# Layer 0's denominators and normed tokens turned in 32x32 squares, and its projection put off by one block

## The chip, the cores and the metric

The kernel runs on one core of one Trainium2 chip. Its engines are PE (TensorE: matmuls and the transposes that go through PSUM), DVE (VectorE), ACT (ScalarE), POOL (GpSimd) and SP, which here only issues DMAs. The metric is the device time of one execution in microseconds (us).

## The reference, cut to what matters

The input is x of 4 images, 128 channels, 64 x 64 pixels: 4 x 128 x 4096 in float32. Layer 0 is an attention over pixels with 64 inner channels, layer 1 a causal attention over the same 4096 tokens with 128 channels, and then a recurrence over the tokens.

```python
# layer 0, per image, xf = x.reshape(128, 4096)
q, k, v = wq @ xf, wk @ xf, wv @ xf                  # 64 x 4096 each
att = softmax(k.T @ q, axis=-1)                      # 4096 x 4096
x = x + wo @ (att @ v.T).T
# layer 1, tokens t = x.T (4096 x 128)
n = layernorm(t)
t = t + softmax(causal((n Wq) (n Wk).T / sqrt(128))) (n Wv)
w = batchnorm(layernorm(t) W)                        # statistics over all images and tokens
y[0] = 0;  y[i] = sigmoid(w[i] + y[i-1] V.T);  t = t + y
```

## The kernel before, in words

Batch by batch (b, the image), layer 0 and then layer 1 go over 8 blocks g of 512 rows of the attention (tokens). For each block the keys are walked in items, two 128-key tiles at a time: 16 items for each block of layer 0, 2 to 16 for a block of layer 1. The main loop (L822) has one slot s per item. In a slot stand, in this order of the program text: `scores` of item s (PE into the PSUM tile s_ps, two buffers; ACT then writes the exponentials p, four buffers), `values` of item s-2 (PE adds p times v, or times the normed tokens, into acc, one buffer), some work at a block's end, `sums` of item s (DVE adds p into dsum, the running denominators), and one piece of work that is due. The scores and values of layer 0 are matmuls on quarters of the array (64 x 64), those of layer 1 use the whole of it (128 x 128).

At a block's last `values` ACT copies acc out (half), DVE adds its parts up to agg (128 x 512, the unnormalized result) and folds dsum into den (128 x 512, keys in partitions, still to be summed over the partitions). Then the loop calls `rows` (L812: takes the query rows for the block after the next: L533 on PE and L535 on DVE for layer 1, a token load on SP for layer 0), pops one entry of the list `fill` (L836), and pushes the block's finishing chain, `finish0` or `finish1`, onto `waiting`. A chain is a generator: each of its steps yields after how many slots it is due, and one due step is taken in a slot (L841), the longest due first. Where none is due, a step of `side` (keys and values of the next batch) is taken. The order on each engine is then fixed when the program is built; the planner that does it may move an instruction past others that don't depend on it, so the order of the trace isn't always that of the text.

Finishing a block of layer 0 takes: `project` (L538), which turns den into one reciprocal per token (rec), multiplies agg by wo on PE (o_ps, L562) and adds it, times rec, to the tokens in xs (four instructions on DVE, L567); `normed` (L571), the layernorm of four token tiles on DVE with a power on POOL (L450), into xh; and `transposed` (L587), which turns xh into xhT, channels in partitions, by four PE transposes (L591) and an ACT copy (L592). In `project` layer 0 turns den with four PE transposes (L557) and reduces them from PSUM (L558). Layer 1 does the same by 32x32 squares: one DVE transpose of all squares (L546), a reduce within the squares (L548, part), a matmul with the 0/1 matrix fold that adds the four partition groups (L549), and on DVE a product with the mask quarter and a reduce (L551, L554). PSUM tiles of `project`, `rows`, the keys and `transposed` share one tag, misc, with two buffers.

Layer 1 finishes in three steps, `first` (project, store of the tokens into x2, norm), `second` (the normed tokens turned on DVE in squares, L640, stored into DRAM as by_c by four DMAs, L645, and loaded as xhT by one, L649) and `third` (the matmul with wf, L653). Tiles agg and den live in the pool `work` (two buffers each).

Layer 0's tokens xhT and xh are what layer 1's `scores` and `values` multiply with: block g's are first read by `rows` and `scores` of layer 1's block g.

Of the kernel before, what the change touches and what calls it, by code (L numbers as in the profile page):

```python
# [9 lines left out]
F32 = mybir.dt.float32  # L10
AF = mybir.ActivationFunctionType
ALU = mybir.AluOpType
AX = mybir.AxisListType
PSUM = bass.MemoryType.PSUM

P = 128
BLK = 512
# [332 lines left out]
def fast_path(  # L350
# [21 lines left out]
    nc = tc.nc  # L372
# [5 lines left out]
    TPB = BLK // P  # L378
# [5 lines left out]
    S = nc.vector.STREAM_SQUARE_SIZE  # L384
    Q = P // S
# [4 lines left out]
    dram2 = ctx.enter_context(tc.tile_pool(name="dram2", bufs=2, space=bass.MemoryType.DRAM))  # L390
# [31 lines left out]
    ident = const.tile([P, P], F32, name="ident")  # L422
# [10 lines left out]
    fold = const.tile([P, P], F32, name="fold")  # L433
# [6 lines left out]
    quarter = const.tile([P, TPB, Q], F32, name="quarter")  # L440
# [15 lines left out]
    with tc.tile_pool(name="batch", bufs=1) as batch, tc.tile_pool(name="rows", bufs=2) as rowp, tc.tile_pool(  # L456
        name="prob", bufs=4
    ) as prob, tc.tile_pool(name="work", bufs=2) as wk, tc.tile_pool(name="stat", bufs=4) as stat, tc.tile_pool(
        name="ps_s", bufs=2, space=PSUM
    ) as ps_s, tc.tile_pool(name="ps_a", bufs=1, space=PSUM) as ps_a, tc.tile_pool(  # L460
        name="ps_m", bufs=2, space=PSUM
# [12 lines left out]
        bs = [Batch() for _ in range(B)]  # L474
# [60 lines left out]
            nc.vector.tensor_copy(r, ps)  # L535
            bs[b].next.append(r)

        def project(layer, b, g, agg, den):  # L538

            dp = misc("den_ps")  # L540
            rec = recs[:, layer, b, ts(g, TPB)]
            if layer:


                sq = wk.tile([P, TPB * Q, S], F32, tag="sq", name="sq")
                nc.vector.transpose(out=sq.rearrange("p a b -> p (a b)"), in_=den)  # L546
                part = stat.tile([P, TPB * Q], F32, tag="part", name="part")
                nc.vector.tensor_reduce(part, sq, AX.X, ALU.add)  # L548
                nc.tensor.matmul(dp[:, : TPB * Q], lhsT=fold, rhs=part, start=True, stop=True)  # L549
                own = stat.tile([P, TPB, Q], F32, tag="own", name="own")  # L550
                nc.vector.tensor_tensor(  # L551
                    own, dp[:, : TPB * Q].rearrange("p (j q) -> p j q", q=Q), quarter, ALU.mult
                )
                nc.vector.tensor_reduce(rec, own, AX.X, ALU.add)  # L554
            else:
                for j in range(TPB):
                    nc.tensor.transpose(dp[:, ts(j, P)], den[:, ts(j, P)], ident)  # L557
                nc.vector.tensor_reduce(rec, dp.rearrange("p (j k) -> p j k", k=P), AX.X, ALU.add)  # L558
            nc.vector.reciprocal(rec, rec)
            op = misc("o_ps")  # L560
            for j in range(TPB):
                nc.tensor.matmul(  # L562
                    op[:, ts(j, P)], lhsT=agg[:, ts(j, P)], rhs=wv1 if layer else wo2, start=True, stop=True
                )
            for j in range(TPB):
                t = xs[:, b, ds(g * BLK + j * P, P)]
                nc.vector.scalar_tensor_tensor(  # L567
                    t, in0=op[:, ts(j, P)], scalar=rec[:, j : j + 1], in1=t, op0=ALU.mult, op1=ALU.add
                )
# [17 lines left out]
        def transposed(src, dst, name, engine):  # L587

            ps = misc(name)
            for j in range(TPB):  # L590
                nc.tensor.transpose(ps[:, ts(j, P)], src[:, j], ident)  # L591
            engine(dst, ps)  # L592

        def in_range():

            r = recs.rearrange("p l b t -> p (l b t)")
            r2 = wk.tile([P, BLK], F32, tag="den", name="r2")[:, : 2 * B * NT]
            nc.vector.tensor_scalar(r2, r, LOW, None, ALU.is_ge)
            nc.vector.tensor_scalar(r, r, HIGH, None, ALU.is_le)
            nc.vector.tensor_tensor(r, r, r2, ALU.mult)  # L600
            nc.vector.tensor_reduce(good, r, AX.X, ALU.add)

        def finish0(b, g):

            agg, den = bs[b].agg, bs[b].den

            def norm():
                if g == 0:
                    bs[b].xh = batch.tile([P, NT, P], F32, tag="xh", name="xh")
                    bs[b].xhT = batch.tile([P, N], F32, tag="xhT", name="xhT")  # L610
                normed(b, g, bs[b].xh[:, ts(g, TPB)])

            yield 2, lambda: (project(0, b, g, agg, den), norm())
            fill.append(
                lambda: transposed(bs[b].xh[:, ts(g, TPB)], bs[b].xhT[:, ts(g, BLK)], "xhT_ps", nc.scalar.copy)
            )

        def finish1(b, g):
            agg, den = bs[b].agg, bs[b].den
            mem = {}  # L620
            final = b == B - 1 and g == NB - 1

            def first():
                project(1, b, g, agg, den)
                nc.sync.dma_start(
                    out=x2[b, ts(g, BLK)].rearrange("(j p) c -> p j c", p=P),
                    in_=xs[:, b, ts(g, BLK)].rearrange("p (j c) -> p j c", c=P),
                )
                mem["xh"] = wk.tile([P, TPB, P], F32, tag="xh2", name="xh2")
                normed(b, g, mem["xh"])  # L630

            def second():
                mem["xhT"] = wk.tile([P, BLK], F32, tag="xhT2", name="xhT2")
                if final:
                    transposed(mem["xh"], mem["xhT"], "xh2T_ps", nc.vector.tensor_copy)
                    return


                sq = wk.tile([P, Q, TPB, S], F32, tag="sqT", name="sqT")
                nc.vector.transpose(  # L640
                    out=sq.rearrange("p c j t -> p j c t"), in_=mem["xh"].rearrange("p j (c r) -> p j c r", r=S)
                )
                by_c = dram2.tile([Q, S, Q, P], F32, tag="by_c", name="by_c")
                for q in range(Q):
                    nc.sync.dma_start(  # L645
                        out=by_c[:, :, q].rearrange("c r k -> r c k"),
                        in_=sq[ts(q, S)].rearrange("r c j t -> r c (j t)"),
                    )
                nc.sync.dma_start(out=mem["xhT"], in_=by_c.rearrange("c r q k -> (c r) (q k)"))  # L649

            def third():
                wp = misc("wx_ps")
                nc.tensor.matmul(wp, lhsT=wf, rhs=mem["xhT"], start=True, stop=True)  # L653
                if b == B - 1 and g == NB - 1:
                    in_range()
                nc.vector.bn_stats(stats[:, b * NB + g], wp)  # L656

                to = xs[:, b, ts(g, BLK)]
                if final:
                    nc.scalar.copy(to.rearrange("p (s c) -> p s c", c=CPB), wp.rearrange("p (c s) -> p s c", s=STEPS))  # L660
                else:
                    nc.scalar.copy(  # L662
                        to.rearrange("p (s j q u) -> p s j q u", q=Q, j=TPB, s=STEPS),
                        wp.rearrange("p (q j u s) -> p s j q u", q=Q, j=TPB, s=STEPS),
                    )

            yield 1, first
            yield 3, second
            yield 1 if final else 4, third
# [121 lines left out]
        fill = []  # L791

        def push(slot, chain):
            step = next(chain, None)
            if step:
                waiting.append((slot + step[0], step[1], chain))
# [25 lines left out]
        for s in range(len(items) + SKEW + 16):  # L822
            if s < len(items):
                it = items[s]
                if it.first:
                    bs[it.b].rows = bs[it.b].next.pop(0)
                    if it.layer and it.g == 1 and it.b + 1 < B:
                        for m in range(NB // 2):
                            side += keys(it.b + 1, m)
                scores(it)  # L830
            if 0 <= s - SKEW < len(items):
                it = items[s - SKEW]
                values(it)
                if it.last:
                    rows()
                    if fill:  # L836
                        fill.pop(0)()
                    push(s, (finish1 if it.layer else finish0)(it.b, it.g))
            if s < len(items):
                sums(items[s])  # L840
            due = [w for w in waiting if w[0] <= s]  # L841
            if due:
                w = min(due, key=lambda w: w[0])
                waiting.remove(w)
                w[1]()
                push(s, w[2])
            elif side:
                side.pop(0)()
# [7 lines left out]
    with tc.tile_pool(name="xr", bufs=1) as xrp, tc.tile_pool(name="y", bufs=2) as yp, tc.tile_pool(  # L856
        name="ps_y", bufs=1, space=PSUM
# [21 lines left out]
        start = xrp.tile([P, B, NCH + 1], F32, name="start")  # L879
# [55 lines left out]
        for b in range(B):  # L935
# [3 lines left out]
            sq = yp.tile([P, NCH], F32, tag=f"y{b}", name="sq")  # L939
# [70 lines left out]
```

## Time and profile before

| | |
|---|---|
| median of 8 runs | 2144.36 us (2142.72 to 2146.3) |
| the profiled execution | 2142.87 us, span 2141.1 us, granted clock 0.994 |
| PE busy | 2093.4 us (98%) |
| DVE busy | 1467.0 us (69%) |
| ACT busy | 1008.4 us (47%) |
| four den transposes on PE, L557 | 128, 20.8 us busy |
| four token transposes on PE, L591 | 128, 20.4 us busy |
| reduce of the denominators from PSUM, L558 | 32, 21.9 us busy |
| copy of the tokens out of PSUM, L592 | 32, 19.0 us busy (ACT) |

The profile is that of one execution. Busy time is the time in which an engine has at least one instruction running; matmuls overlap, so the sum of their lengths is more than PE's busy time. A line of the timeline has the start in us, the length in us, the engine, the line of the kernel, the operation, the tiles written and read, the number of like instructions merged, and in brackets the time that the engine stood idle before it and which instruction ended that.

### The profile page before, as it was taken

What the parts mean: (1) busy time and instruction counts of PE and PEld (TensorE: products, weight loads), DVE (VectorE), ACT (ScalarE), POOL (GpSimd) and SP (SyncE); (2) the same over time, 40 slices, a digit from 0 to 9 for tenths busy, and PEclk for the clock granted to TensorE, in tenths of its full rate; (3) what the DMA queues carried; (4) which work ended last, traced back from release to release, by engine and by line L of the source; (5) the groups of instructions that cost most, each with busy time, mean ns of one, the idle gap of its engine ahead of it and who ended that gap; (6) DMA issues with size and microseconds to landing.
All of it is one profiled execution on the core that took longest, in us unless ns stands there. A gap on an engine that the chain in (4) does not pass through costs nothing. (4 is left out here: it accounts for less than half of the span.)

```text
span 2141.1 us, 30417 instructions
## 1 busy us (share of the span) xinstructions
PE 2093.4 (98%) x12016; PEld 925.6 (43%) x12016; DVE 1467.0 (69%) x2807; ACT 1008.4 (47%) x1098; POOL 104.2 (5%) x207
## 2 busy tenths in 40 slices
PE   6999999999999999999999999999999999999978
PEld 2333344444333344444333334444433334544446
DVE  3888875554788876554588887555488887654478
ACT  4666633333566643333466663333356664323255
POOL 0000010000000000000000001000000001000000
PEclk9999999999999999999999999999999999999989
DMA  7000022000000002100000002200000000110033
GB/s 227 2 1 2 1 60 57 18 15 15 16 1 1 2 18 71 35 25 15 16 1 2 1 1 59 59 15 15 15 16 1 1 2 6 40 30 15 15 162 159
DMA packets 65319, 64.99 MB, mean 30 GB/s; under 512 B 5648, under 2 KB 55056, under 8 KB 63120
## 3 DMA queue, kind: packets, MB, share of 16 engines
q1 hardware_dynamic: 63280, 62.41, 9.8%
q8 instruction: 96, 1.57, 0.3%
q10 hardware_dynamic: 1888, 0.56, 0.1%
q14 instruction: 55, 0.45, 0.1%
HBM read 33.85 MB, written 24.90 MB: 27 GB/s over the span
## 5 line engine op out<-in xcount | busy, mean ns | idle before, releaser
L744 DVE TENSOR_TENSOR dsum<-dsum,p 128x1024 f32<-128x1024 f32 x676 | 827.1, 1224 | 446.3 <-ACT p L720 320.4
L718 ACT ACTIVATE p<-s_ps,nshift 128x1024 f32<-128x1024 f32 x512 | 571.2, 1116 | 348.7 <-PE s_ps L704 328.8
L720 ACT ACTIVATE p<-s_ps 128x1024 f32<-128x1024 f32 (+2 forms) x288 | 274.2, 952 | 564.2 <-PE s_ps L713 542.5
L764 PE MATMUL acc<-p,v 64*64 64x512 f32 x4096 | 533.6, 591 | 1.7 <-ACT half L783 1.7
L704 PE MATMUL s_ps<-swap,kr 64*64 64x512 f32 x2048 | 529.2, 594 | 0.4 <-ACT p L718 0.4
L704 PE MATMUL s_ps<-kr 64*64 64x512 f32 x2048 | 529.2, 594 | 0.0
L713 PE MATMUL s_ps<-rows,xhT 128*128 128x512 f32 (+3 forms) x1152 | 503.3, 559 | 1.4 <-DVE rows L535 1.4
L772 PE MATMUL acc<-p,xh 128*128 128x512 f32 (+3 forms) x1152 | 501.7, 558 | 0.0
L772 PEld LDWEIGHTS acc<-p,xh 128*128 128x128 f32 x1152 | 216.2, 191 | 240.8 <-issue 231.4
L713 PEld LDWEIGHTS s_ps<-rows,xhT 128*128 128x128 f32 x1152 | 213.4, 190 | 241.9 <-issue 196.1
L764 PEld LDWEIGHTS acc<-p,v 64*64 64x64 f32 x4096 | 155.5, 133 | 285.1 <-issue 266.1
L704 PEld LDWEIGHTS s_ps<-swap,kr 64*64 64x64 f32 x2048 | 137.5, 133 | 132.8 <-issue 125.1
L704 PEld LDWEIGHTS s_ps<-kr 64*64 64x64 f32 x2048 | 137.6, 133 | 128.3 <-issue 123.7
L450 POOL TENSOR_TENSOR ln_rstd<-ln_var,mhalf 128x4 f32<-128x4 f32 x64 | 65.7, 1027 | 1205.0 <-DVE ln_var L579 1194.1
L752 DVE TENSOR_TENSOR dsum<-dsum,p 128x256 f32<-128x256 f32 (+1 forms) x120 | 55.8, 499 | 74.2 <-POOL p L724 74.2
L567 DVE SCALAR_TENSOR_TENSOR xs<-o_ps,recs,xs 128x128 f32<-128x128 f32 x256 | 72.4, 344 | 8.8 <-PE o_ps L562 3.1
L583 DVE TENSOR_SCALAR xh<-xs,ln_mv,ln_rstd 128x128 f32<-128x128 f32 x256 | 71.3, 342 | 2.2
L724 POOL TENSOR_SCALAR_AFFINE_SELECT p<-p 128x128 f32<-128x128 f32 x128 | 34.4, 292 | 665.6 <-ACT p L720 650.8
L576 DVE BATCH_NORM_STATS2 ln_st<-xs 128x6 f32<-128x128 f32 x256 | 63.5, 270 | 0.0
L742 DVE COPY dsum<-p 128x1024 f32<-128x1024 f32 x60 | 41.4, 690 | 31.8 <-ACT p L720 26.6
L662 ACT COPY xs<-wx_ps 128x512 f32<-128x512 f32 x31 | 18.1, 585 | 83.7 <-DVE stats L656 79.1
L909 DVE SCALAR_TENSOR_TENSOR z<-xs,scale,y_ps 128x256 f32<-128x256 f32 x108 | 48.6, 480 | 6.7 <-PE y_ps L907 5.5
(115 smaller groups left out, 1047.1 us busy)
## 6 DMA issues: line engine op xcount, KB each, us to landing
xs<-in_x SPq DMA_DIRECT2D x16, 512.0 KB, 7.3
xs<-in_xT SPq DMA_DIRECT2D x32, 256.0 KB, 3.2
x<-xs SPq DMA_DIRECT2D x32, 256.0 KB, 2.3
xr<-x SPq DMA_DIRECT2D x8, 1024.0 KB, 11.9
out_x<-xr SPq DMA_DIRECT2D x8, 1024.0 KB, 6.0
by_c<-sqT SPq DMA_DIRECT2D x124, 64.0 KB, 1.8
xhT<-by_c SPq DMA_DIRECT2D x31, 256.0 KB, 2.6
swap<-kr SPq DMA_DIRECT2D x32, 128.0 KB, 2.2
```

Of the source, the lines that this page charges most:

```text
L450: nc.gpsimd.tensor_tensor(y, var, mhalf[:, : y.shape[-1]], ALU.pow)
L567: nc.vector.scalar_tensor_tensor(t, in0=op[:, ts(j, P)], scalar=rec[:, j : j + 1], in1=t, op0=ALU.mult, op1=ALU.add)
L576: nc.vector.bn_stats(st[:, j], xs[:, b, ds(g * BLK + j * P, P)])
L583: nc.vector.tensor_scalar(dst[:, j], xs[:, b, ds(g * BLK + j * P, P)], mv[:, j, 0:1], y[:, j : j + 1], ALU.subtract, ALU.mult)
L704: nc.tensor.matmul(ps[c * M : c * M + M, off : off + n], lhsT=bs[it.b].kr[part, h, ds(t % (NT // 2) * P + c * M, M)], rhs=rows[h], start=True,
L713: nc.tensor.matmul(ps[:, off : off + n], lhsT=lhsT, rhs=rhs, start=True, stop=True)
L718: nc.scalar.activation(it.p[:, :off], ps[:, :off], AF.Exp, bias=nshift)
L720: nc.scalar.activation(it.p[:, :off], ps[:, :off], AF.Exp, scale=float(P) ** -0.5)
L744: nc.vector.tensor_tensor(flat, flat, it.p, ALU.add)
L752: nc.vector.tensor_tensor(den[:, h, q0:], den[:, h, q0:], it.p[:, o : o + n], ALU.add)
L764: nc.tensor.matmul(bt.acc[h * M : h * M + M, r], lhsT=bt.v[part, t], rhs=it.p[part, o : o + n], start=it.first, stop=it.last,)
L772: nc.tensor.matmul(bt.acc[:, 0, q0:], lhsT=bt.xh[:, t], rhs=it.p[:, o : o + n], start=it.first and h == 0, stop=it.last and h == 1,)
```

## The change

Layer 0 takes over layer 1's way of turning. `project` has one form for both layers, and its first half, the DVE transpose of den in squares and the reduce to part, becomes a function of its own, `folded`. The normed tokens of a layer-0 block are no more transposed by PE: DVE turns their 32x32 squares (`squares`, the code that layer 1 had in its `second`), four DMAs on SP's queue put these into a DRAM tile by_r (pieces of 32 tokens, 128 bytes), and four more load the rows of xhT from it.

The steps of `finish0` stand elsewhere. Before: project and norm together, due two slots behind the block's end, and the transposes at the next block's end (the entry in `fill`). After: `folded` due one slot behind the block's end; project at the next block's end (the entry in `fill`), and from there a new chain: norm due one slot later, `by_channels` (squares and the eight DMAs) two after that. At a block's end the chain of the block before is pushed ahead of the block's own. `finish1` calls the same functions with the same work as before.

```diff
+        def folded(den):
+            sq = wk.tile([P, TPB * Q, S], F32, tag="sq", name="sq")
+            nc.vector.transpose(out=sq.rearrange("p a b -> p (a b)"), in_=den)
+            part = stat.tile([P, TPB * Q], F32, tag="part", name="part")
+            nc.vector.tensor_reduce(part, sq, AX.X, ALU.add)
+            return part
+
-        def project(layer, b, g, agg, den):
+        def project(layer, b, g, agg, part):
             dp = misc("den_ps")
             rec = recs[:, layer, b, ts(g, TPB)]
-            if layer:
...
-            else:
-                for j in range(TPB):
-                    nc.tensor.transpose(dp[:, ts(j, P)], den[:, ts(j, P)], ident)
-                nc.vector.tensor_reduce(rec, dp.rearrange("p (j k) -> p j k", k=P), AX.X, ALU.add)
+            nc.tensor.matmul(dp[:, : TPB * Q], lhsT=fold, rhs=part, start=True, stop=True)
+            own = stat.tile([P, TPB, Q], F32, tag="own", name="own")
+            nc.vector.tensor_tensor(own, dp[:, : TPB * Q].rearrange("p (j q) -> p j q", q=Q), quarter, ALU.mult)
+            nc.vector.tensor_reduce(rec, own, AX.X, ALU.add)
             nc.vector.reciprocal(rec, rec)
...
+        def squares(src):
+            sq = wk.tile([P, Q, TPB, S], F32, tag="sqT", name="sqT")
+            nc.vector.transpose(out=sq.rearrange("p c j t -> p j c t"), in_=src.rearrange("p j (c r) -> p j c r", r=S))
+            return sq
...
-            yield 2, lambda: (project(0, b, g, agg, den), norm())
-            fill.append(
-                lambda: transposed(bs[b].xh[:, ts(g, TPB)], bs[b].xhT[:, ts(g, BLK)], "xhT_ps", nc.scalar.copy)
-            )
+            def by_channels():
+                sq = squares(bs[b].xh[:, ts(g, TPB)])
+                by_r = dram2.tile([S, Q, TPB, Q, S], F32, tag="by_r", name="by_r")
+                for q in range(Q):
+                    nc.sync.dma_start(
+                        out=by_r[:, :, :, q].rearrange("r c j t -> r (c j) t"),
+                        in_=sq[ts(q, S)].rearrange("r c j t -> r (c j) t"),
+                    )
+                for c in range(Q):
+                    nc.sync.dma_start(
+                        out=bs[b].xhT[ts(c, S), ts(g, BLK)], in_=by_r[:, c].rearrange("r j q t -> r (j q t)")
+                    )
+
+            def rest():
+                yield 1, norm
+                yield 2, by_channels
+
+            def first():
+                part = folded(den)
+
+                def second(s):
+                    project(0, b, g, agg, part)
+                    push(s, rest())
+
+                fill.append(second)
+
+            yield 1, first
...
-                project(1, b, g, agg, den)
+                project(1, b, g, agg, folded(den))
...
-                        fill.pop(0)()
+                        fill.pop(0)(s)
```

More of the change, by code (lines that the diff above doesn't have):

```diff
@@ L536, in rows1 @@
             bs[b].next.append(r)
-        def project(layer, b, g, agg, den):
+        def folded(den):
[5 more added lines that the diff above has]
+        def project(layer, b, g, agg, part):
             dp = misc("den_ps")
             rec = recs[:, layer, b, ts(g, TPB)]
-            if layer:
[L545 to L552, printed above, removed]
-                )
-                nc.vector.tensor_reduce(rec, own, AX.X, ALU.add)
-            else:
-                for j in range(TPB):
-                    nc.tensor.transpose(dp[:, ts(j, P)], den[:, ts(j, P)], ident)
-                nc.vector.tensor_reduce(rec, dp.rearrange("p (j k) -> p j k", k=P), AX.X, ALU.add)
+            nc.tensor.matmul(dp[:, : TPB * Q], lhsT=fold, rhs=part, start=True, stop=True)
+            own = stat.tile([P, TPB, Q], F32, tag="own", name="own")
+            nc.vector.tensor_tensor(own, dp[:, : TPB * Q].rearrange("p (j q) -> p j q", q=Q), quarter, ALU.mult)
+            nc.vector.tensor_reduce(rec, own, AX.X, ALU.add)
             nc.vector.reciprocal(rec, rec)
@@ L611, in norm @@
                 normed(b, g, bs[b].xh[:, ts(g, TPB)])
-            yield 2, lambda: (project(0, b, g, agg, den), norm())
-            fill.append(
-                lambda: transposed(bs[b].xh[:, ts(g, TPB)], bs[b].xhT[:, ts(g, BLK)], "xhT_ps", nc.scalar.copy)
-            )
+            def by_channels():
[20 more added lines that the diff above has]
+            yield 1, first
         def finish1(b, g):
@@ L636, in second @@
                     return
[L639 to L642, printed above, removed]
+                sq = squares(mem["xh"])
                 by_c = dram2.tile([Q, S, Q, P], F32, tag="by_c", name="by_c")
```

## The prediction

> **What bounds the kernel now.** I read the page's engine totals first, then the busy time per stretch, then PE, DVE and ACT in order of time through one layer-0 block end, then the same for layer 1, where the new form of the denominators already runs.
>
> The engine totals, and one layer-0 block of 16 items in the view of stretches (span, then PE, PEld, DVE, ACT, POOL busy, clock, DMA share, GB/s):
>
> ```profile
> PE 2093.4 (98%) x12016; PEld 925.6 (43%) x12016; DVE 1467.0 (69%) x2807; ACT 1008.4 (47%) x1098; POOL 104.2 (5%) x207
> 182.20:212.04 29.84, 29.84 (x274) 11.36 (x273) 24.98 (x41) 19.19 (x19) 1.01 (x1) 1.00 0.01 1
> ```
>
> PE never stops in the block, at full granted clock; DVE, 69% of the whole, is 84% busy here. So the two have to be set against each other per block, and not over the span.
>
> PE in order of time around a block end (start us, length, engine, line):
>
> ```profile
> 89.67 1.04 PE L764 MATMUL acc<-p,v 64*64 64x512 f32 x8
> ...
> 91.38 1.04 PE L764 MATMUL acc<-p,v 64*64 64x512 f32 x8
> 92.35 0.66 PE L591 MATMUL xhT_ps<-ident,xh 128*128 128x128 f32 x4
> ...
> 93.85 1.04 PE L764 MATMUL acc<-p,v 64*64 64x512 f32 x8
> ...
> 95.56 1.04 PE L764 MATMUL acc<-p,v 64*64 64x512 f32 x8
> 96.53 0.66 PE L557 MATMUL den_ps<-ident,den 128*128 128x128 f32 x4
> 97.03 1.06 PE L562 MATMUL o_ps<-wo,agg 128*128 128x128 f32 x8
> ...
> 98.92 1.04 PE L764 MATMUL acc<-p,v 64*64 64x512 f32 x8
> ```
>
> A plain slot takes 1.716 us (ACT's starts, 220.31 to 239.19, are eleven slots). The slot with the token transposes takes 2.47, so these cost PE 0.75. The slot with denominators and projection takes 3.36, so these cost 1.64, of which 0.98 is the projection (97.03 to 98.01, where the scores go on). Sixteen slots of 1.716 (27.46) and 2.39 make 29.85: nothing else is in the period, and PE sets it.
>
> DVE in the same kind of block (in brackets the idle time before, and its releaser):
>
> ```profile
> 210.03 0.69 DVE L788 TENSOR_TENSOR den<-dsum 128x512 f32<-128x512 f32 x1
> ...
> 212.20 1.23 DVE L744 TENSOR_TENSOR dsum<-dsum,p 128x1024 f32<-128x1024 f32 x1 [0.87 <-ACT p L718]
> ...
> 214.67 1.23 DVE L744 TENSOR_TENSOR dsum<-dsum,p 128x1024 f32<-128x1024 f32 x1 [0.64 <-ACT p L718]
> 216.38 1.23 DVE L744 TENSOR_TENSOR dsum<-dsum,p 128x1024 f32<-128x1024 f32 x1 [0.49 <-ACT p L718]
> ...
> 222.09 0.16 DVE L451 TENSOR_TENSOR ln_z<-ln_rstd 128x4 f32<-128x4 f32 x1 [1.12 <-POOL ln_rstd L450]
> ...
> 224.93 13.21 DVE L744 TENSOR_TENSOR dsum<-dsum,p 128x1024 f32<-128x1024 f32 x10
> 238.63 1.23 DVE L744 TENSOR_TENSOR dsum<-dsum,p 128x1024 f32<-128x1024 f32 x1 [0.49 <-ACT p L718]
> ```
>
> The idle times add to 3.61, so DVE needs 26.25 of 29.86. The ten sums back to back show it 3.5 us behind ACT (the sum at 224.93 takes a p that ACT ended at 221.42), catching up 0.4 us a slot (1.716 less 1.32).
>
> **What is removed and added, on PE.** In layer 1 the fold and the projection look so, with the transpose of the normed tokens on DVE:
>
> ```profile
> 397.93 0.29 PE L549 MATMUL den_ps<-part,fold 128*128 128x16 f32 x2
> 398.07 1.14 PE L562 MATMUL o_ps<-wv,agg 128*128 128x128 f32 x8
> ...
> 405.18 0.71 DVE L640 STREAM_TRANSPOSE sqT<-xh 128x512 f32<-128x512 f32 x1
> 405.81 1.18 DVE L744 TENSOR_TENSOR dsum<-dsum,p 128x1024 f32<-128x1024 f32 x1
> ```
>
> The fold takes 0.14 of PE there, with its weight loads hidden. Behind 64x64 work both loads (0.19 each) may show: 0.38 at most. I take 0.20, nearer the measured one. The moved projection stays 0.98. Going into 128x128 work shows 0.11 (96.42, the end of the eight L764 at 95.56 plus 0.86, to 96.53), and the first scores after it take 0.05 more; two such visits a block become one. New: 0.11 + 0.20 + 0.98 + 0.05 = 1.34 against 2.39: 1.05 us saved a block, period 28.80. Seven of a batch's eight blocks pay in layer 0: 28 x 1.05 = 29.4. The eighth is dealt with among layer-1 work, where four transposes cost 0.44 (299.86 to 300.30; 283.72 to 284.16): 0.44 + 0.44 - 0.14 = 0.74, times 4 = 3.0. Together 32.4 us.
>
> The token transposes also covered PE's wait for the copy of acc at a block end (0.42 idle at 63.94, the first block, where there are none). The projection, 1.34 long, now stands there, so that stays covered.
>
> **PSUM buffers of the misc tag (two).** At a batch's last two layer-0 ends the rows of layer 1 (L533) take one, den_ps the other, and o_ps must wait until DVE has copied the rows: in the trace the rows matmul is over at 242.59, the copy at 243.88. With o_ps straight behind, PE waits 1.1 (243.9 less 242.8). Where this happens today, the order steps around it: at 283.72 den_ps, then scores at 284.16, then o_ps at 285.67; here that costs one more visit, 0.16. Between 0.16 and 1.1, nearest the stepping around: 0.3, eight times, 2.4 us.
>
> **What is added on DVE.** Squares and reduce of den, 0.74 + 0.69 (430.45 to 431.19, and the reduce); own and its reduce 0.41 (398.69 to 399.10); squares of the tokens 0.63 (above); less the reduce from PSUM, 0.72 (98.10 to 98.82). Plus 1.75: 28.00 a block, inside PE's 28.80, if it waits for nothing. But DVE waits for POOL's power in every norm. Near the end of layer 0, where DVE is behind:
>
> ```profile
> 1827.45 1.22 DVE L744 TENSOR_TENSOR dsum<-dsum,p 128x1024 f32<-128x1024 f32 x1
> 1829.57 0.16 DVE L451 TENSOR_TENSOR ln_z<-ln_rstd 128x4 f32<-128x4 f32 x1 [0.90 <-POOL ln_rstd L450]
> 1827.62 1.91 POOL L450 TENSOR_TENSOR ln_rstd<-ln_var,mhalf 128x4 f32<-128x4 f32 x1 [9.56 <-DVE ln_var L579]
> ```
>
> A sum put into that wait began 0.17 before the power, which took 1.91 instead of 1.01, and DVE stood 0.90 all the same. Where the power began first (401.92, sum at 402.10) it took 1.01 and no wait was left. With DVE behind, the next p is always ready, so the sum will begin first: I charge 0.90 a block, 1.12 if nothing is put in. DVE: 28.90 to 29.12, above PE by 0.10 to 0.32.
>
> [...]
>
> Does that excess reach PE? There are four p buffers: ACT writes item k+4 once DVE has summed item k, 6.86 us after item k's start; less ACT's 1.12 and the sum's 1.29, DVE may be 4.45 late before ACT waits, and ACT has 1.4 to spare before PE does: 5.85. The new lag, from the end of the last p of a block (0): last sum 1.26, den 0.61, copy 0.69, squares and reduce 1.43, sum 1.14, agg 0.69, own to the four updates 1.72, sum 1.22, statistics 1.41, sum 1.22, 0.90, chain and xh 1.70, sum 1.30, squares 0.63 = 15.9; the p then due ended at 11.6 (6 x 1.716 + 1.34). Lag 4.3 to 4.5, under 5.85; the spare 1.4 takes up most of seven drifts of 0.10 to 0.32. What is left is 0 to 1.2 a batch: 0 to 5 us, I take 2.
>
> **Queues and the delay.** ACT loses 32 copies of 0.59: off the path. SP gets eight DMAs a block: four stores at 0.44 (1.76 for the like four), four loads at 0.34, 3.1 of 28.8. Behind them on SP stand the token loads two blocks ahead, the x2 stores and by_c; the loads wait there for the stores to land. The nearest store (64 KB in 512 B pieces) lands in 1.8; with pieces of 128 B, four times as many, 1.8 to 7.2 each. Block 0's xhT is read five blocks later, so this is hidden. What could be late is layer 1's first by_c behind block 6's stores: these start near 286, and in series at 7.2 land by 315, where by_c now starts at 301.08; its data, now there by 307, would come at 321, 4 behind their use at 316.8. So 0 to 4 a batch, 0 to 17 us; I take 0, as stores near the measured 1.8 are done by 294. [...] Agg is held one block longer; of its two buffers the older is freed at the next block's end, a block before the third is wanted, so nothing waits.
>
> **Sum.** 32.4 - 2.4 - 2 = 28.0. Profiled execution 2142.87 (span 2141.1) gives 2114.9; the median of the runs lies 1.5 above it: 2116.4.
>
> **Rivals.**
> - DVE becomes the pace, with a gain left: it keeps the POOL wait (0.90 or 1.12) and a 0.49 before a sum. Period 29.39 to 29.61, saved 28 x 0.25 to 0.47, plus 3: 10 to 16, about 2131. For: 28.90 leaves no slack. Against: DVE behind has its inputs ready. 12%.
> - Slower, by the same engine in a fixed order that makes it wait. It decides at 1.86 idle a block (29.86 less 28.00). POOL 1.12, a wait for o_ps as at 286.76 (0.66), and the 0.64 and 0.49 that a wrong order keeps make 2.91: 30.9, or 28 x 1.05 = +29: 2171 with the 3 taken off. For: DVE's order is fixed ahead, and the projection now comes right behind agg, which waits for ACT. Against: in layer 1 the squares fill gaps (430.45 right behind den). 22%.
> - Late layer-1 inputs through SP: 17 us given back, 2133. Against: SP is empty. 4%.
> - Nothing to measure, PE's gain and DVE's new waits cancelling (idle of 1.6 to 2.1): 2144. 5%.
>
> **How the numbers follow.** My forecast, 57%: its own range is 2110 (fold 0.14, PSUM and DVE free) to 2131 (fold 0.38, 1.1 eight times, DVE 5). Of this kernel 0.2%, 4.3 us, is about what can be told from no change. Faster: 57 + 12 + 4 = 73%; same 5%; slower 22%. The range: 2105, leaving little below, to 2152, which takes in the lighter half of the slower case.
>
> **What would show it.** Right: layer-0 periods of 28.8 to 29.1; L549 twice as many, no L557 and L591 but the last block's; PE without gaps in layer 0. DVE near 27 busy of 29. Wrong: PE idle or ACT waiting on dsum in layer 0 (the p buffers), periods over 29.86, o_ps waiting for the rows copy, or wx waiting for by_c.

## The result and the profile after

The changed kernel takes 2139.09 us (median of 11 runs, 2135.84 to 2143.81) where the kernel before, timed beside it, takes 2144.48 (2142.22 to 2147.8): ratio 0.9972, 95% interval 0.9964 to 0.998. The gain is 5.4 us; 28 were forecast. The profiled execution is 2139.59 us, its span 2137.9, its granted clock 0.991 (before: 0.994).

The engine totals of the page after:

```profile
PE 2077.0 (97%) x11824; PEld 911.6 (43%) x11824; DVE 1521.5 (71%) x2935; ACT 992.3 (46%) x1066; POOL 103.0 (5%) x207
```

PE lost 16.4 us of busy time and DVE gained 54.5. So PE has less to do, and only a third of that shows in the time. One layer-0 block in the view of stretches (columns as in the prediction):

```profile
149.12:178.60 29.48, 29.17 (x268) 10.77 (x268) 26.62 (x46) 18.76 (x18) 1.01 (x1) 1.00 0.09 19
```

Before, PE was busy for all of the 29.84; now it stands idle for 0.31 of a shorter block. Something else sets the period. I measured the periods of layer 0 from copy to copy of acc (starts of `half` on ACT, in us). First batch, blocks 1 to 7:

| | | | | | | | | sum |
|---|---|---|---|---|---|---|---|---|
| before | 29.76 | 29.86 | 29.85 | 29.86 | 29.86 | 29.85 | 31.77 | 210.81 |
| after | 28.12 | 28.94 | 29.26 | 29.48 | 29.48 | 29.83 | 35.18 | 210.29 |

Two things stand in this row. The plain blocks settle at 29.48, not at the forecast 28.8 to 29.1. And the last period is 3.4 us longer than before and takes nearly all of the gain back; in the four batches it is 35.18, 35.21, 33.57 and 35.18.

PE in order of time around a plain block end after (start, length, engine, line):

```profile
89.67 1.04 PE L787 MATMUL acc<-p,v 64*64 64x512 f32 x8
90.63 0.39 PE L552 MATMUL den_ps<-part,fold 128*128 128x16 f32 x2
90.88 1.14 PE L559 MATMUL o_ps<-wo,agg 128*128 128x128 f32 x8
...
92.85 1.04 PE L787 MATMUL acc<-p,v 64*64 64x512 f32 x8
```

From 89.67 to 92.85 are 3.19 us before rounding; less a plain slot of 1.716, the one visit to 128x128 work costs 1.47 (forecast: 1.34). The fold, 90.63 to 90.88, is 0.25.

DVE through one plain block after:

```profile
147.95 0.69 DVE L811 TENSOR_TENSOR den<-dsum 128x512 f32<-128x512 f32 x1
148.67 0.71 DVE L541 STREAM_TRANSPOSE sq<-den 128x512 f32<-128x512 f32 x1
149.42 0.69 DVE L543 TENSOR_REDUCE part<-sq 128x16 f32<-128x512 f32 x1
...
150.81 1.23 DVE L767 TENSOR_TENSOR dsum<-dsum,p 128x1024 f32<-128x1024 f32 x1
...
155.06 1.19 DVE L767 TENSOR_TENSOR dsum<-dsum,p 128x1024 f32<-128x1024 f32 x1
...
157.68 0.16 DVE L451 TENSOR_TENSOR ln_z<-ln_rstd 128x4 f32<-128x4 f32 x1 [1.12 <-POOL ln_rstd L450]
...
159.62 0.71 DVE L594 STREAM_TRANSPOSE sqT<-xh 128x512 f32<-128x512 f32 x1
160.26 17.14 DVE L767 TENSOR_TENSOR dsum<-dsum,p 128x1024 f32<-128x1024 f32 x13
177.43 0.69 DVE L811 TENSOR_TENSOR den<-dsum 128x512 f32<-128x512 f32 x1
```

From den to den are 29.48 us, and in all of them the only wait is the 1.12 for POOL's power. Thirteen sums stand back to back up to the block's end: in this block DVE never catches up. (In the block behind it, one of 29.83, it does once, and waits 0.46 for a p at 203.34.) DVE is the pace of these blocks, with 29.48 - 1.12 = 28.36 us of its own (forecast: 28.00).

The other engines hear of it through the p buffers. In the groups of waits of ACT (total us, times, longest), this one is new:

```profile
ACT p L741 <- DVE dsum L767: 52.9, 63, 2.6
```

Now the last period. The same place, the sixth block end of a batch, in PE's order of time, first before:

```profile
241.63 1.13 PE L533 MATMUL r_ps<-xhT,g 128*128 128x512 f32 x2
242.59 0.60 PE L591 MATMUL xhT_ps<-ident,xh 128*128 128x128 f32 x4
243.12 0.65 PE L704 MATMUL s_ps<-kr 64*64 64x512 f32 x2
...
246.72 0.66 PE L557 MATMUL den_ps<-ident,den 128*128 128x128 f32 x4
247.22 1.05 PE L562 MATMUL o_ps<-wo,agg 128*128 128x128 f32 x8
```

and after:

```profile
237.62 1.12 PE L533 MATMUL r_ps<-xhT,g 128*128 128x512 f32 x2
238.58 0.29 PE L552 MATMUL den_ps<-part,fold 128*128 128x16 f32 x2
238.80 1.07 PE L727 MATMUL s_ps<-kr 64*64 64x512 f32 x2
241.48 1.98 PE L559 MATMUL o_ps<-wo,agg 128*128 128x128 f32 x8 [1.61 <-DVE rows L535]
```

Before, two slots of scores and values lay between the rows and the projection, and the second misc buffer was free by then. After, r_ps and den_ps hold both buffers, o_ps needs the one that DVE's copy of the rows gives back, and PE stands for 1.61 us with the scores queued behind o_ps. Why the copy is late is on DVE:

```profile
236.73 0.69 DVE L811 TENSOR_TENSOR den<-dsum 128x512 f32<-128x512 f32 x1
...
239.60 1.23 DVE L767 TENSOR_TENSOR dsum<-dsum,p 128x1024 f32<-128x1024 f32 x1
240.74 0.68 DVE L535 COPY rows<-r_ps 128x512 f32<-128x512 f32 x1
```

r_ps was complete at about 238.7. DVE was still busy with den, its squares, a copy and a sum, and came to the rows only at 240.74.

The wait isn't the whole price. The view of stretches behind it (the clock is the third column from the end):

```profile
240.00:242.00 2.00, 0.52 (x3) 0.53 (x4) 2.00 (x4) 0.00 (x0) 0.00 (x0) 0.90 0.00 0
242.00:244.00 2.00, 2.00 (x11) 1.46 (x14) 0.96 (x6) 0.00 (x0) 0.00 (x0) 0.50 0.00 0
244.00:246.00 2.00, 2.00 (x20) 0.58 (x16) 1.35 (x8) 0.68 (x1) 0.00 (x0) 0.74 0.00 0
```

When PE goes on, it does so at half clock: o_ps took 1.98 where the one at 90.88 took 1.14. The clock lost (0.10 + 0.50 + 0.26) x 2 = 1.7 us. In the third batch the same wait of 1.61 was followed by full clock:

```profile
1254.00:1256.00 2.00, 0.39 (x2) 0.01 (x1) 1.90 (x4) 0.00 (x0) 0.00 (x0) 1.00 0.00 0
1256.00:1258.00 2.00, 2.00 (x19) 1.33 (x22) 1.78 (x8) 0.00 (x0) 0.00 (x0) 1.00 0.00 0
```

and there the last period is 33.57 instead of 35.2. So the half clock is worth 1.6 us of a period; of the 1.8 that are left of the excess over the period before, 1.61 is the wait. How the waits that half clock followed lay against the others stands in the last section.

### The profile page after: what moved, and what is told of

Its sections match the earlier page's. It is cut to its first block, busy times and chain, and to the rows that moved or that the text cites. A ratio compares the mean times of both kernels' runs of the same rounds, so it can differ in the third digit from the quotient of the medians.

```text
span 2137.9 us, 30557 instructions
## 1 busy us (share of the span) xinstructions
PE 2077.0 (97%) x11824; PEld 911.6 (43%) x11824; DVE 1521.5 (71%) x2935; ACT 992.3 (46%) x1066; POOL 103.0 (5%) x207
## 3 DMA queue, kind: packets, MB, share of 16 engines
HBM read 42.24 MB, written 33.29 MB: 35 GB/s over the span
## 5 line engine op out<-in xcount | busy, mean ns | idle before, releaser
L787 PE MATMUL acc<-p,v 64*64 64x512 f32 x4096 | 575.2, 592 | 1.7 <-ACT half L806 1.7
L727 PE MATMUL s_ps<-kr 64*64 64x512 f32 x2048 | 572.1, 594 | 4.8 <-ACT p L741 4.8
L787 PEld LDWEIGHTS acc<-p,v 64*64 64x64 f32 x4096 | 169.4, 134 | 283.6 <-issue 275.7
L727 PEld LDWEIGHTS s_ps<-kr 64*64 64x64 f32 x2048 | 153.5, 133 | 144.9 <-issue 124.6
```

What stands on the lines that cost most here:

```text
L727: nc.tensor.matmul(ps[c * M : c * M + M, off : off + n], lhsT=bs[it.b].kr[part, h, ds(t % (NT // 2) * P + c * M, M)], rhs=rows[h], start=True,
L787: nc.tensor.matmul(bt.acc[h * M : h * M + M, r], lhsT=bt.v[part, t], rhs=it.p[part, o : o + n], start=it.first, stop=it.last,)
```

## The experiments

Two suspects: four p buffers with a late DVE (the periods of 29.48), and the rows of layer 1 in front of the projection (the last period). In the diffs a line with + is the experiment's.

### A fifth p buffer

```diff
-        name="prob", bufs=4
+        name="prob", bufs=5
```

> The changed kernel with five p buffers in place of four; the order on PE, DVE and ACT is the same but for one copy at the end. Theory (two faults: DVE falls further behind at a block end than four p buffers allow, and a PSUM wait at the sixth block end): the layer-0 periods of 29.26 to 29.83 fall to 28.9 to 29.1 and ACT no more waits for dsum, while the long period at the end of layer 0 (35.2) stays; 29.26 + 29.48 + 29.48 + 29.83 less 4 x 29.0 is 2.1 a batch, so 7 to 9 us under the changed kernel, about 2131. Rival (DVE has too much work on average, whatever the buffers): the periods stay at 29.4 or more and the time within 3 us of the changed kernel.

Measured: 2142.97 us, ratio to before 0.9996 (0.9987 to 1.0006). The periods did what the theory says: 28.12, four times 28.94, 29.49. But the last became 38.09 (36.90, 38.07, 36.91 in the other batches), and the kernel is 4 us slower than the changed one. The first theory, that the buffers are what is short, is refuted by DVE in a plain block of this run:

```profile
149.68 0.69 DVE L811 TENSOR_TENSOR den<-dsum 128x512 f32<-128x512 f32 x1
...
159.41 0.16 DVE L451 TENSOR_TENSOR ln_z<-ln_rstd 128x4 f32<-128x4 f32 x1 [1.12 <-POOL ln_rstd L450]
...
161.99 17.14 DVE L767 TENSOR_TENSOR dsum<-dsum,p 128x1024 f32<-128x1024 f32 x13
179.16 0.69 DVE L811 TENSOR_TENSOR den<-dsum 128x512 f32<-128x512 f32 x1
```

From den to den it is 29.48 again, to the hundredth, with PE at 28.94. The buffer only lets PE run ahead, by 0.54 a block, and the lead is lost where PE next needs DVE. At the sixth end:

```profile
243.20 2.08 PE L559 MATMUL o_ps<-wo,agg 128*128 128x128 f32 x8 [3.33 <-DVE rows L535]
```

3.33 us where the changed kernel waits 1.61; den started at 238.45 in place of 236.73, with r_ps at 237.62 in both. All four batches then ran at half clock there.

### The projection ahead of the rows

```diff
-                    rows()
                     if fill:
                         fill.pop(0)(s)
+                    rows()
```

> At a block's end the projection of the block before is put ahead of the rows of layer 1, so that it doesn't wait for a PSUM buffer that the rows hold until DVE has copied them. Theory (two faults): the period from the seventh to the eighth end of a batch falls from 35.2 to about 31, and nothing else changes: 4 x 4.2 = 17 us less, about 2122. Rival (the long period comes from DVE being late, or from the change to layer 1): it stays over 34 and the time within 4 us of the changed kernel.

Measured: 2139.33 us, 0.9978 (0.9969 to 0.9988): no change. The last periods are 33.02, 34.49, 34.67, 34.67. The wait changed its name: now r_ps needs a buffer, and stands 1.96 us at 242.06 for `own`, DVE's read of den_ps. With two buffers and three tiles, one of them waited for a late DVE in both orders.

### Both

The two edits together.

> Five p buffers and the projection ahead of the rows. Theory (two faults, each for itself): both gains add, 2139 - 8 - 17 = 2114, periods 28.9 to 29.1, and the forecast of 2116 is what the change would give without the two waits. Rival (they are one fault seen twice, DVE late): the sum is no better than the better one alone, 2122 or more.

Measured: 2141.68 us, 0.999 (0.998 to 1.0). The forecast of 2114 is missed by far. Last period 37.23 (36.38, 36.38, 36.39), and the wait is

```profile
241.69 2.08 PE L533 MATMUL r_ps<-xhT,g 128*128 128x512 f32 x2 [3.68 <-DVE own L554]
```

Three runs, one reading: whatever stands second at that end pays DVE's lag, and the more PE got ahead before, the more.

### The projection ahead of the rows, norm and squares later

```diff
-                yield 1, norm
-                yield 2, by_channels
+                yield 4, norm
+                yield 4, by_channels
```

> Four p buffers; the projection ahead of the rows, and the norm put off from one to four slots behind it, the tokens' squares four slots behind the norm. Theory (it is the heap of DVE work at the block end, not its amount, that outruns four buffers): the lag of DVE is cut by the norm's 4 us, ACT waits no more for dsum, and the time is that of five buffers with the same order, about 2114. Rival (amount, not heap): as the projection ahead of the rows alone, 2120 to 2124.

Measured: 2147.59 us, 1.0013 (1.0003 to 1.0023), with the projection ahead of the rows as in the run before last. ACT's wait for dsum stayed at 51.9 us (52.9), so spreading DVE's burst in this way doesn't help, which fits that the sum of DVE's work is too long and not its order. The stretch from the last layer-0 block end over layer 1 to the first layer-0 block end of the next batch became 298.9 long (about 296 with the projection ahead alone): 1.7 of the difference is a stretch of half clock at the end of layer 1, which this run has in all three batches and the other in one, and 0.8 is a new PE wait for ACT's agg (at 323.77 in the first batch).

### The rows in the middle of a block

```diff
+                if it.layer == 0 and it.g == NB - 1 and it.k in (8, 10):
+                    rows()
...
-                    rows()
+                    if it.layer or it.g < NB - 2:
+                        rows()
```

> The changed kernel, four p buffers; the rows of layer 1's first two blocks (which stood at the sixth and seventh ends of layer 0, between the projection's two PSUM tiles) are made in the middle of the last layer-0 block, where the two buffers are free and DVE isn't late. In the two runs with the projection ahead of the rows, the rows waited for den_ps in its place (3.68 us at 238.0 in the one with five p buffers), and PE ran at half its clock behind each such wait. Theory (PE stands at that end for a PSUM buffer that late DVE holds, and then pays a second time through the clock): no PE wait over 1 us in layer 0, no half clock, the period from the seventh to the eighth end falls from 35.2 to about 32, the others stay at 29.1 to 29.5: 4 x 3.2 = 13 us less than 2139, 2126. Rival (DVE's lag alone costs this, the buffer is only where it shows): it stays over 34 and the time within 4 us of 2139.

Measured: 2126.59 us, 0.9927 (0.9911 to 0.9944). The projection follows its fold without a wait,

```profile
238.51 0.40 PE L552 MATMUL den_ps<-part,fold 128*128 128x16 f32 x2
238.76 1.14 PE L559 MATMUL o_ps<-wo,agg 128*128 128x128 f32 x8
```

at full clock, and the last period is 32.37. (Of the eight waits that the expectation recalls, seven were followed by half clock, not each; the first one with four buffers was not.) The other periods stay as they were (29.28, 29.48, 29.48, 29.84). One place, the order of two calls at two block ends of eight, is worth 12.5 us of the kernel (12.9 in the second timing). Timed again beside the next one:

> The changed kernel with the rows of layer 1 in the middle of the last layer-0 block, a second time and side by side with the next one, both timed longer, because the first comparison left the worth of the fifth p buffer open (2126.6 and 2123.6, with intervals that overlap). Expected by both readings: 2126, within 2 us, since nothing is changed in it.

Measured: 2126.17 us, 0.9909 (0.9895 to 0.9922).

### The same with a fifth p buffer

> The same with five p buffers. Theory (two separate costs): periods of 28.94 as in the run with five buffers alone, about 31.4 at the end of layer 0: a batch's seven periods are 28.12 + 5 x 28.94 + 31.4 = 204.2 against 210.8 before, 26 us less than 2144: 2118. Rival (what the buffers give is always given back at the end of layer 0, since DVE is only later there): 2124 or more, with the last period at 34 or more.

Measured: 2123.61 us, 0.9905 (0.9889 to 0.9922). Periods 28.12, four times 28.94, 29.50, 32.38. It missed its 2118, and against the neighbour the intervals overlap, so both were run again:

> The same with five p buffers. Theory (ACT waiting for dsum is time lost by the whole kernel): layer-0 periods over 28.94 added up to 8.6 us with four buffers and to 1.5 with five, so 5 to 7 us below its neighbour, 2119 to 2121. Rival (DVE is later at the start of layer 1, and PE's waits and half clock there give it back): within 2 us of its neighbour.

Measured: 2123.43 us, 0.99 (0.9885 to 0.9915): 2.7 below its neighbour, between the two expectations. The layer-0 periods above 28.94 add up to some 8.5 us with four buffers and 1.5 with five; about 7 are gained there and 4 lost again. DVE's den-to-den is 29.46 to 29.48 in most blocks of both. Where some of it returns is seen in PE's waits, in layer 1, first with four buffers:

```profile
PE o_ps L559 <- DVE rows L535: 1.7, 4, 1.1
```

and then with five:

```profile
PE o_ps L559 <- DVE rows L535: 5.2, 4, 2.0
```

This version is the fastest of all, 21 us below the kernel before.

### The kernel before with the rows in the middle of a block

The edit of two sections above, made in the kernel before.

> The kernel before, with only the rows of layer 1's biases moved from the last two layer-0 block ends of a batch into the middle of the last layer-0 block, as in the run that brought the changed kernel from 2139.1 to 2126.6. Theory (the cost at the sixth end belongs to the change: the projection is issued right behind the rows, where the kernel before had scores between them): here nothing is waited for at those ends, so 2144, within 3 us. Rival (the rows cost PE the same in both kernels, and the move is a gain of its own): 2131 to 2134, and then the change itself is worth only 5 us against it.

Measured: 2144.27 us, 0.9993 (0.9984 to 1.0003). The move isn't a gain of its own; its last period is 33.29 (before 31.77), given back in layer 1. So the 12.5 us belong to the change: it made the place dear, and the move made it free again.

### The kernel before with five p buffers

> The kernel before with five p buffers in place of four. Theory (four were enough before, because DVE was only 3.5 us behind at a block end): no group of ACT waiting for dsum to take away, so 2144, within 2 us. Rival (ACT was held there too, in layer 1 or at the first blocks): 2135 or less.

Measured: 2143.96 us, 0.9996 (0.9986 to 1.0005). In layer 0 no ACT wait for dsum was there to be taken away, and nothing is gained: DVE had 3.61 us of idle time in those blocks.

### The denominators alone

In the kernel before, the one form of `project`; projection, norm and the PE transposes of the tokens where they were.

```diff
-            if layer:
...
-            else:
-                for j in range(TPB):
-                    nc.tensor.transpose(dp[:, ts(j, P)], den[:, ts(j, P)], ident)
-                nc.vector.tensor_reduce(rec, dp.rearrange("p (j k) -> p j k", k=P), AX.X, ALU.add)
```

> The kernel before with one part of the change alone: layer 0's denominators by squares, all in one step where they were; tokens through PE as before. By the rows of the changed kernel the fold and projection cost PE 1.47 in a slot in place of 1.64: period 29.7, saved 28 x 0.17 and 4 x 0.3: 6 us, 2138. DVE needs 27.4 and 1.1 of waiting, less than 29.7. Rival (DVE's added 1.1 us at the block end already outruns four p buffers): ACT waits for dsum, and it is not faster.

Measured: 2137.01 us, 0.9968 (0.9957 to 0.9979). PE is still the pace, period 29.69, last period 31.60. The visit to the denominators and the projection:

```profile
96.67 0.40 PE L546 MATMUL den_ps<-part,fold 128*128 128x16 f32 x2
96.91 1.14 PE L555 MATMUL o_ps<-wo,agg 128*128 128x128 f32 x8
...
98.89 1.04 PE L757 MATMUL acc<-p,v 64*64 64x512 f32 x8
```

The fold is 0.24 where four transposes were 0.50 (96.53 to 97.03 in the prediction's lines), but the period fell by 0.17 only. Half the change gives at least as much as all of it (7.2 us against 5.4, each beside its own timing of the kernel before, with overlapping intervals).

### The tokens alone

In the kernel before, the tokens through squares and DRAM, two slots behind the norm; the denominators as before.

```diff
-            fill.append(
-                lambda: transposed(bs[b].xh[:, ts(g, TPB)], bs[b].xhT[:, ts(g, BLK)], "xhT_ps", nc.scalar.copy)
-            )
+            yield 2, by_channels
```

> The kernel before with the other part alone: denominators and projection as before, two slots behind the block's end; the normed tokens by squares through DRAM. PE loses the 0.75 of the token transposes, but at each block end it then waits for the copy of acc, which they covered (0.4 to 0.6): period 29.5 to 29.7, saved 28 x 0.15 to 0.35 and 4 x 0.4: 6 to 11 us, 2133 to 2138. Rival (the small pieces through DRAM delay layer 1): waits for xhT, and no gain.

Measured: 2141.48 us, 0.9986 (0.9977 to 0.9996), a miss. The four transposes cost PE 0.75 a block, and the period fell by 0.10, to 29.76. They had stood in front of PE's wait for the copy of acc, which is now in the open at the ends of plain blocks:

```profile
122.78 1.09 PE L781 MATMUL acc<-p,v 64*64 64x512 f32 x8 [0.42 <-ACT half L800]
```

0.42 of the 0.75 is that wait (10.1 us, 24 times, in the groups); with the 0.10 gained, 0.23 is left without a name. The kernel before showed it already: its first period, which holds no token transposes, is 29.76 too. So moving the projection to that place was needed for the tokens to pay more than 0.10, as the prediction's line on the cover has it; it is the same move that met the rows.

## Why the prediction was wrong

The direction was right, the size not: 2116.4 forecast, 2139.1 measured, inside the range and outside the forecast's own. By its steps:

**PE's saving: nearly right.** 1.34 was forecast for the new visit, 1.47 measured: the fold took 0.25 for 0.20, and the projection 1.06 (90.88 to 91.94, where the scores go on) for 0.98. PE's own period, seen where DVE doesn't hold it, is 28.94 (forecast 28.80). With five buffers the layer-0 periods of the four batches lie 27.0 us below those of the kernel before, rows in the middle of a block in both (forecast: 29.4). Most of what PE was to save in layer 0 was there to be had. One thing was counted in the wrong place: the seven periods hold six of the new visits, not seven, as the projection of the seventh block, put off by a block, falls at the eighth end, among layer-1 work. By the prediction's own terms that is 1.64 + 6 x 1.05, 31.8 us in four batches, saved in layer 0, and nothing in layer 1, where it has 3.0.

**DVE's work: the failed step, which stands behind the next two.** The prediction took 26.25 = 29.86 - 3.61 for what DVE needs, and added 1.75. Measured is 28.36, 0.36 more. The working shows why: four of the five idle times in the 3.61 stand in front of sums, and a sum of 1.23 that follows another starts 1.33 after it (17.14 for thirteen). The 0.10 between the two was counted as idle time; 4 x 0.10 is about the 0.36. In these blocks DVE was never free and paid it. With POOL's wait of 1.12, which stayed empty, DVE needs 29.48, not 28.90 to 29.12, and is 0.54 a block slower than PE in place of 0.10 to 0.32. The rival "DVE becomes the pace" had 29.39 to 29.61 by another sum, and the measured 29.48 lies in it; it was given 12%. The 0.49 in its sum didn't come in the blocks of 29.48, so the period that it hit is luck; its 2131 fails mostly on what follows.

**"The excess reaches PE late": the limits were right, the lag wasn't.** At 189.74 DVE sums a p that ACT ended at 183.61, 6.1 late (forecast 4.3 to 4.5), and the ACT instruction that wants the buffer comes 1.64 late: the limit of 4.45 holds. PE lost 0.54 of that, so its spare was 1.1, not 1.4. Two sums stood inside the burst, not four, and DVE began it late. Charged were 2 us; the fifth buffer is worth 2.7 to 3.0 once the last period is mended.

**The PSUM buffers: right place, wrong size, and the dearest error.** The prediction named the wait, o_ps for the rows copy, and the eight ends. It priced it "between 0.16 and 1.1" and took 0.3, since the order had stepped around it in layer 1. In layer 0 it didn't: one pair of scores was put between, and o_ps in front of the rest. Nor is 1.1 an upper bound: it takes the copy as coming right behind the rows, with a DVE that is free, and the late DVE made it 1.61 (3.33 with five buffers). And no term stood for the clock behind the wait. Forecast 2.4 us; measured, by taking it away, 12.5. Four of the eight ends count: at the others, among layer-1 work, the wait is 0.44 (at 275.78).

**SP and the DMAs: right.** They cost nothing that shows on PE: no wait of PE's is for by_r, and its waits for by_c add to 5.7 us (6.1 before). ACT waits for xhT from by_r three times, 6.6 us in all, off the path. In the view of DMA issues (KB each, median us to landing):

```profile
by_r<-sqT SPq DMA_DIRECT2D x128, 64.0 KB, 2.2
xhT<-by_r SPq DMA_DIRECT2D x128, 64.0 KB, 2.0
by_c<-sqT SPq DMA_DIRECT2D x124, 64.0 KB, 1.8
```

Stores in pieces of 128 bytes (by_r) land in 2.2, 0.4 above the 1.8 of the like store in pieces of 512 (by_c), and far from 7.2, the upper end of the author's estimate.

**The ledger.** 28.0 forecast, 5.4 measured, 22.6 missing. The sixth ends took 12.5 for 2.4: 10.1. The p buffers took 2.7 to 3.0 for 2: about 1. The other 11.5 lie between the best version, 2123.5, and 2112.0, the forecast without those two terms. 2.4 of them are missing in layer 0 (29.4 less 27.0; 1.5 of that are the periods above 28.94). 3.8 are PE's work in the stretch over layer 1. PE's projections of layer 0 from the first batch's last copy of acc to the next batch's first (busy us behind the bar), before and after:

```profile
L562 PE MATMUL o_ps<-wo,agg 128*128 128x128 f32 x8 | 1.1, 275 | 0.0
L559 PE MATMUL o_ps<-wo,agg 128*128 128x128 f32 x16 | 2.2, 281 | 0.4 <-DVE rows L535 0.4
```

The second eight are the seventh block's, worth 1.1; with the folds, and without the transposes, PE's work in this stretch is 0.2 longer, where the prediction has it 0.74 shorter. Of the 5.3 that are left, most are the 5.2 of waits for the rows above: the lag that DVE takes along out of layer 0 is paid in layer 1. This was read from the traces and not isolated by a run, and the kernel before, timed four more times, came out between 2143.8 and 2145.6, so the ledger isn't good to better than a us or two. The stretches over layer 1 differ by up to 2 us from batch to batch in one trace, 1.7 of it half clock.

The slower rival (2171) and the cancelling one (2144) didn't come, but the changed kernel was nearer to the second than to the forecast: gain and new waits did largely cancel, in the last period, by a mechanism that the prediction had at 2.4 us.

## What to carry to other kernels

When work moves onto an engine that is 84% busy, take what it needs from a stretch in which it runs without a pause (start to start), not from the span less its idle times: here four gaps of 0.10 us between instructions were counted as idle time and came back, as about 0.36 us a block, when the idle time was gone. Once two engines are that close, look for the places where the faster one needs the slower one's answer (here a PSUM buffer), and price them with the slower one late; a fifth p buffer alone only moved the wait there, 3.33 us for 1.61. A call order at a block end whose move gained nothing in the kernel before (2144.27) was the dearest line of the change, 12.5 us: try such a line in another place before giving the change up.

## What the runs showed of the hardware

From 60 to 2000 us PE's clock fell to half behind waits of 1.6 to 3.7 us (1.61 in the changed kernel, 3.68 with both edits), for 3.41 us at a time (6.8 behind three of the longest), in the changed kernel in the middle of work that had run at full clock for 191 us or more. The same wait of 1.61, in the same place, was followed by it in three batches of four; waits of 3.3 (the fifth p buffer) and 3.7 (both edits) in eight of eight. The kernel before shows it too, behind a wait of 2.35 us at 1061, and not behind two of 1.9 at 554 and 1570, so the state is not the change's own; the change only brought four more occasions.

The waits can be set beside the record of the granted clock. In the changed kernel the stretches of half clock begin at 241.62, 555.64, 750.21 and 1760.55, which are 92, 57 and 296 steps of 3.413 us apart; in the kernel before at 1062.73 and 2049.18, 289 such steps apart. In the first batch the whole wait lies in the step before 241.62; in the third the wait (1254.38 to 1255.99) is cut in two by the end of a step, 0.99 and 0.62, and the clock stays:

```profile
238.21:241.62 3.41, 1.80 (x7) 0.66 (x6) 3.31 (x5) 0.70 (x1) 0.00 (x0) 1.00 0.00 0
1251.96:1255.37 3.41, 2.42 (x10) 0.86 (x6) 3.26 (x5) 1.46 (x2) 0.20 (x1) 1.00 0.00 0
1255.37:1258.79 3.42, 2.80 (x24) 1.63 (x28) 3.20 (x13) 0.57 (x1) 0.00 (x0) 1.00 0.00 0
```

In the traces of the two kernels, cut from 60 to 2000 us into such steps, those at full clock that half clock followed held 1.61 (three of them), 1.86 and 2.11 us of idle PE. Of the other steps at full clock two in the kernel before held 1.85 and 1.72, and none held more than 1.06 beside these. What makes the clock fall was not shown. The wait of 1.61 cost some 3.2 us where half clock followed: its own length, and the 1.6 by which the third batch's period was shorter.

On DVE a sum that follows a sum (both write dsum) started 1.33 us after it, and another instruction that followed one and had nothing to wait for 1.14, as from 150.81 to 151.95 above (medians of 285 and 137 such pairs in the changed kernel). In thirteen sums in a row that is 12 x 0.19 = 2.3 us a block, by estimate, of the engine that sets the period; no run here tried to part them.
